# Mixture-of-experts blocks of 256 with a last block of 128 for experts that have at most 128 choices left

## The chip, the cores and the metric

The kernel runs on one core of a Trainium2 chip. The metric is device time in microseconds (us), the median of the runs shown. Before the change it is 2036.22 us, the median of three runs (2031.78, 2036.22 and 2037.07).

## The reference, cut to what matters

The network has four layers over 2708 nodes (rows of `x`) with 256 features each. Every layer is a graph step (a weighted sum over neighbours through the 2708 x 2708 matrix `adj`) followed by a feed-forward step. The change is in the feed-forward step of layer 0, a mixture of eight experts:

```python
def _L0_ffn_ref(x, Wg, bg, W1, b1, W2, b2):
    TOP_K = 2
    xf = x.reshape(-1, D)
    gate_logits = xf @ Wg + bg
    top_w, top_i = jax.lax.top_k(gate_logits, TOP_K)
    top_w = jax.nn.softmax(top_w, axis=-1)
    w_dense = jnp.sum(jax.nn.one_hot(top_i, E, dtype=xf.dtype) * top_w[..., None], axis=1)
    out = jnp.zeros_like(xf)
    for e in range(E):
        h = jax.nn.gelu(xf @ W1[e] + b1[e], approximate=False)
        out = out + w_dense[:, e:e + 1] * (h @ W2[e] + b2[e])
    return out.reshape(B, L, D)

# --- layer 0 ---
x = x + _L0_gnn_ref(_layernorm(x), adj, L0_gnn_W, L0_gnn_B)
x = x + _L0_ffn_ref((_layernorm(x))[None], L0_ffn_Wg, ...)[0]
# --- layer 1 ---
x = x + _L1_gnn_ref(_layernorm(x), adj, L1_gnn_W, L1_gnn_b)
...
```

Each row chooses two of the eight experts, so there are 2 x 2708 = 5416 choices, each of which needs one expert's two products (256 to 1024, gelu, 1024 to 256). Which expert gets how many choices depends on the data. The inputs come from a fixed seed. Layer 1's feed-forward step has one common hidden layer and lets every row choose one expert for the second product.

## The kernel before

Everything is float32. One matrix product of a 128 x 128 stationary tile is written as two TensorE instructions in the trace, so the 16 products of an expert block's first layer appear as 32 instructions.

**Layer 0's graph step** goes over the rows in three groups of 9, 7 and 6 tiles of 128 (`GROUPS`). After each group `send` normalizes its rows, computes the gate, chooses two experts per row, and `route` gives every choice a place in a list in memory (`taken0`) that is sorted by expert within the group. The rows, with their place in the output and their weight, are scattered to these places by indirect DMAs from GpSimd's queue.

**Planning.** `blocks` turns the counts per expert into a list of blocks. A block belongs to one expert and holds `B` of its choices (`B` = 256 in layer 0, two halves `k` of 128). For each block it computes the expert's number `ei` and, for every lane, the place `ix` in `taken0` from which its row is read. It is some thirty small VectorE instructions on all 128 partitions. It is called twice. Call "A" comes after the second group and makes `NA` = 9 blocks that are full with what is known by then. Call "B" (line 899) comes after the third group and makes `MOST - NA` = 20 blocks for the rest; the last block of each expert is filled up with lanes that point out of range, and their reads and writes are dropped. A 256-row block with 8 rows in it takes as much time as a full one.

**The expert stage.** `work0.run(hc, items, ...)` (line 935) is unrolled over the 9 blocks of "A" and the first `ALWAYS` = 15 blocks of "B". For each block:

- `fetch` (SyncE's queue) loads the two weight matrices of the block's expert, `wa` and `wb`, two blocks ahead; there are three buffers for each.
- `fetch_rows` (GpSimd's queue) gathers the two halves' rows into `xs`, three blocks ahead; for blocks of "B" VectorE first sets `xs` to ones.
- `turn` transposes the rows on TensorE (four transposes, line 545) and VectorE copies the result to `xTs` (line 551).
- The first layer: for each of 8 slices `f` of the hidden layer two products with 256 columns (line 578) and one gelu on ScalarE over 256 columns (line 580) into `hTs`, of which there is one buffer.
- The second layer: for each half `k`, 8 products with 256 columns (line 587), then bias and weight on VectorE (lines 589, 590), then a scatter of the 128 rows to `given0` from GpSimd's queue (line 481).

`beside(n)` puts other work between the blocks: sums of the columns of `adj`, which layer 1 needs (half rows `adhalf` are loaded on SyncE's queue and added on VectorE, line 925). At block 12 it also loads the number of blocks needed into a register on every engine (`blocks_left`).

`work0.run_rest` (line 937) then holds the five remaining blocks of "B" in a run-time `If`: they are computed only if more than 15 blocks of "B" are needed. After it come the column sums' product (line 942) and layer 1, whose first loads (`both`, line 991) wait until all scatters to `given0` have landed.

**The order of the work** on each engine is set by a scheduler that orders instructions by their place in the source and by when their inputs are free; a few dependencies written by hand ("order") hold things back. Instructions in the `If` are scheduled as one piece. [...]

The change also touches `run_rest` and the count for layer 1 (lines 1142 to 1159), where the blocks have 128 choices and nothing else changes.

Of the kernel before, what the change touches and what calls it, by code (L numbers as in the profile page):

```python
# [8 lines left out]
F32 = mybir.dt.float32  # L9
# [6 lines left out]
P = 128  # L16
N = 2708
# [49 lines left out]
def adj_ffn4(ctx: ExitStack, tc: tile.TileContext, a: dict, out: bass.AP):  # L67
# [326 lines left out]

    def blocks(pool, brief, known, NB, B, name, done=None, full=False):

# [114 lines left out]
    class Blocks:  # L511
# [15 lines left out]
        def fetch_rows(self, item):  # L527
            (_, ix, _), b, past, src, full = item
# [11 lines left out]
        def turn(self, pool, xs, after=None):  # L540
            xT = pool.tile([P, DC, 2 * P], F32, name="xTs", bufs=2)
            p = pools["psum"].tile([P, W], F32, name="turned", bufs=1)
            for k in range(2):
                for c in range(DC):
                    i = te.transpose(p[:, (c * 2 + k) * P : (c * 2 + k + 1) * P],
                                     xs[:, k, c * P : (c + 1) * P], ident)
                    if after is not None:
                        tc.add_manual_dep(i.ins, after, mybir.DependencyInfo(
                            mybir.DependencyClass.NoSync, mybir.DependencyReason.DATA),
                            reason="order")  # L550
            v.tensor_copy(xT.rearrange("p c t -> p (c t)"), p)
            return xT

        def run(self, pool, items, during=None, after=None):
# [9 lines left out]
            for n in range(len(items)):  # L564
                w1, bias, w2 = ahead.pop(0)
                xs, xT = self.rows.pop(0), turned
                if rows_todo:
                    self.fetch_rows(rows_todo.pop(0))
                if todo:
                    self.fetch(todo.pop(0))  # L570
                if during is not None:
                    during(n)
                hT = pool.tile([P, HC, 2 * P], F32, name="hTs", bufs=1)
                for f in range(HC):
                    if f % 2 == 0:
                        p = ps_acc().rearrange("p (k t) -> p k t", k=2)
                    for c in range(DC):
                        te.matmul(p[:, f % 2, :], lhsT=w1[:, c, f * P : (f + 1) * P],  # L578
                                  rhs=xT[:, c, :], start=(c == 0), stop=(c == DC - 1))
                    s.activation(hT[:, f, :], p[:, f % 2, :], AF.Gelu, bias=bias[:, f : f + 1])  # L580
                if self.rows:
                    turned = self.turn(pool, self.rows[0])
                y = pool.tile([P, 2, D], F32, name="ys", bufs=2)
                q = pools["psum"].tile([P, 2, D], F32, name="yacc", bufs=2)
                for k in range(2):
                    for f in range(HC):
                        te.matmul(q[:, k, :], lhsT=hT[:, f, k * P : (k + 1) * P], rhs=w2[:, f, :],  # L587
                                  start=(f == 0), stop=(f == HC - 1))
                    v.tensor_tensor(y[:, k, :], q[:, k, :], w2[:, HC, :], ALU.add)  # L589
                    v.tensor_scalar(y[:, k, :], y[:, k, :], xs[:, k, D + 1 :], None, op0=ALU.mult)  # L590
# [3 lines left out]
        def run_rest(self, pool, items, left, most):  # L594

            with tc.If(left > most):
                self.run(pool, items)
            pin(scattered[self.ok][-1].name)

    class Units(Blocks):  # L600
# [13 lines left out]
        def fetch_names(self, item):  # L614
            (_, ix, _), b, past, src, full = item
            m = self.names[:, self.places[0], :]
# [38 lines left out]
        def run(self, pool, items, during=None):  # L655
# [6 lines left out]
            while self.rows:  # L662
# [56 lines left out]
    held = sum(rows(t) for q in GROUPS[:-1] for t in q)  # L719
    NA, MOST = 9, (2 * N - E) // (2 * P) + E  # L720
    assert NA <= -(-(2 * held - E * (2 * P - 1)) // (2 * P))
    ALWAYS = 15
    with ExitStack() as l0:
# [102 lines left out]
        for tiles in GROUPS:  # L826
# [82 lines left out]
        halves = [(j, c0) for j in range(NT) for c0 in (0, N // 2)]  # L909

# [5 lines left out]
        def beside(b):  # L916


            if b == NA + 3:
                left.append(blocks_left(rest[2], MOST))  # L920
            while read:
# [4 lines left out]
            if b < 3:  # L926
                return
            while halves and len(read) < (3 if b < NA else 2):
                j, c0 = halves.pop(0)
                ad = hp.tile([P, N // 2], F32, name="adhalf", bufs=3)  # L930
# [4 lines left out]
        work0.run(hc, items, beside, gated[-3])  # L935
        assert not halves and not read
        work0.run_rest(hc, more, left[0], ALWAYS)

# [22 lines left out]
    with ExitStack() as l1:  # L961
# [104 lines left out]
        for tiles in GROUPS1:  # L1066
# [82 lines left out]
        def beside(b):  # L1149
            if b == NA + 4:  # L1150
                left.append(blocks_left(rest[2], MOST))
                as_bc = row_bc(work, "L2_gnn_attn_src", D, "elu_e")
# [5 lines left out]
        work1.run(hc, items, beside)  # L1158
        work1.run_rest(hc, more, left[0], ALWAYS)

# [570 lines left out]
```

## Time and profile before

One execution was profiled. Times of stages come from that execution.

| what | value |
|---|---|
| median of the runs | 2036.22 us |
| the profiled execution's own time | 2048.93 us |
| its span in the trace | 2047.2 us |
| TensorE busy | 1916.4 us (94%) |
| VectorE busy | 1103.8 us (54%) |
| first to last gelu of layer 0's experts (line 580) | 275.1 to 623.2 us |
| blocks in that stage | 24 (24 loads of `wa`, 192 gelus of 128 x 256) |
| indirect DMAs in it | 48 gathers into `xs`, 48 scatters to `given0` |
| granted TensorE clock, mean | 0.967 |

How to read it: in a timeline a row gives the start, the time, the engine, the line, the operation, output<-inputs and how many instructions it stands for. PE is TensorE's products, PEld its loading of the stationary tile, DVE VectorE, ACT ScalarE, POOL GpSimd, SPq SyncE's queue of DMAs. In brackets stands how long the engine was idle before and what ended that. The mean time of one product in the groups is a latency; products overlap, so a pace is read from the distance between starts.

### The profile page before, as it was taken

The numbers are of one execution on the slowest core, as the hardware profiler recorded it, in microseconds if no ns is written. First come the engines' busy times: TensorE is split into PE (matmuls) and PEld (weight loads), VectorE is DVE, ScalarE is ACT, GpSimd is POOL, SyncE is SP. The second block draws the span as 40 slices with busy tenths as digits, with TensorE's granted clock in tenths as the row PEclk, the third lists the DMA queues.
The fourth block names the chain that finished last, engine by engine and source line by source line (L and its number), as shares of the span: only waits on it lengthen the run. The fifth ranks groups of instructions, "written<-read, shape, count | busy, mean of one in ns | idle before, by whom it ended". The sixth has DMA issues, their size and how long they took to land.

```text
span 2047.2 us, 25961 instructions
## 1 busy us (share of the span) xinstructions
PE 1916.4 (94%) x9641; PEld 1374.6 (67%) x9641; DVE 1103.8 (54%) x2503; ACT 639.0 (31%) x1407; POOL 333.0 (16%) x369
## 2 busy tenths in 40 slices
PE   7999979999997999999796889999999999999997
PEld 5888868888886788878675768887576522232334
DVE  7687842543434333344341165555445588987876
ACT  8777722222224203022221152223234400120112
POOL 1004362333321000102345300000000000000000
PEclk9999979999998999999897999999899999999998
DMA  8435567877744343534666720000101000000000
GB/s 267 144 101 156 171 219 269 324 289 303 268 175 126 119 137 111 144 86 121 200 200 234 304 69 1 1 1 1 41 1 32 16 1 21 21 26 11 16 11 24
DMA packets 86960, 243.93 MB, mean 119 GB/s; under 512 B 17151, under 2 KB 40919, under 8 KB 77612
## 3 DMA queue, kind: packets, MB, share of 16 engines
q1 hardware_dynamic: 69596, 196.81, 29.0%
q0 software_dynamic: 17232, 45.38, 6.5%
q8 instruction: 79, 1.29, 0.3%
q14 instruction: 53, 0.43, 0.1%
HBM read 216.54 MB, written 28.97 MB: 120 GB/s over the span
## 4 chain that ended last, share of the span: by engine, by line
PE 55%; issue 5%; DMA 5%; DVE 4%; POOL 3%; ACT 2%; POOLq 0%; SPq 0%; DVEq 0%; ACTq 0%
PE num L1643 11%; PE ps_acc L1319 9%; PE acc L1124 8%; PE ps_tmp L347 7%; PE den L1654 6%; PE ps_acc L1495 3%; PE ps_tmp L241 3%; DMA given<-ys,xs 2%; PE ps_tmp L198 1%; PE ps_acc L241 1%; PE ps_tmp L1045 1%; POOL given L481 1%; POOL names L495 1%; PE yacc L674 1%; DMA adrow<-in_adjT 1%
## 5 line engine op out<-in xcount | busy, mean ns | idle before, releaser
L1638 DVE SCALAR_TENSOR_TENSOR e<-arena,G,mask 128x1024 f32<-128x1024 f32 (+2 forms) x264 | 294.2, 1150 | 41.1 <-PE den L1654 40.7
L1643 PE MATMUL num<-e,wh 128*64 128x512 f32 (+4 forms) x1056 | 240.9, 553 | 0.3 <-ACT L_gnn_W L1176 0.3
L1124 PE MATMUL acc<-sup,adrow 128*128 128x256 f32 x882 | 200.7, 385 | 2.8 <-DVE o L1076 1.5
L1319 PE MATMUL ps_acc<-hh,e 128*128 128x257 f32 x882 | 199.2, 382 | 2.0 <-ACT o L1264 2.0
L863 PE MATMUL acc<-msg,wt 128*128 128x256 f32 x882 | 198.1, 381 | 2.4 <-DVE x L886 1.2
L1124 PEld LDWEIGHTS acc<-sup,adrow 128*128 128x128 f32 x882 | 166.4, 192 | 31.0 <-issue 4.6
L578 PE MATMUL ps_acc<-xTs,wa 128*128 128x256 f32 x768 | 179.5, 387 | 6.1 <-issue 3.3
L863 PEld LDWEIGHTS acc<-msg,wt 128*128 128x128 f32 x882 | 165.2, 190 | 28.1 <-DVE wt L824 2.1
L1319 PEld LDWEIGHTS ps_acc<-hh,e 128*128 128x128 f32 x882 | 163.7, 190 | 29.6 <-ACT o L1264 5.0
L1643 PEld LDWEIGHTS num<-e,wh 128*64 128x64 f32 (+1 forms) x1056 | 73.9, 136 | 153.2 <-issue 119.9
L587 PE MATMUL yacc<-wb,hTs 128*128 128x256 f32 x768 | 175.5, 381 | 0.5 <-DVE ys L589 0.5
L580 ACT ACTIVATE hTs<-ps_acc,wa 128x256 f32<-128x256 f32 x192 | 90.8, 475 | 259.4 <-PE yacc L587 172.0
L578 PEld LDWEIGHTS ps_acc<-xTs,wa 128*128 128x128 f32 x768 | 142.1, 192 | 35.2 <-ACT hTs L580 5.3
L587 PEld LDWEIGHTS yacc<-wb,hTs 128*128 128x128 f32 x768 | 145.2, 191 | 20.3 <-DVE ys L589 0.9
L1654 PE MATMUL den<-e,wh 128*32 128x512 f32 (+4 forms) x1056 | 138.2, 553 | 0.0
L1313 DVE SCALAR_TENSOR_TENSOR e<-Rb,G,mask 128x640 f32<-128x640 f32 (+2 forms) x110 | 85.2, 775 | 92.8 <-PE ps_acc L1319 92.7
L199 ACT COPY xT<-ps_tmp 128x256 f32<-128x256 f32 x120 | 40.7, 364 | 276.5 <-PE ps_tmp L198 275.4
L1093 DVE TENSOR_SCALAR mask<-adrow 128x1024 uint8<-128x1024 f32 (+1 forms) x66 | 41.4, 630 | 134.5 <-DMA adrow<-in_adjT 134.5
L674 PE MATMUL yacc<-wb,hTs 128*128 128x256 f32 x384 | 94.7, 400 | 7.6 <-DVE ys L675 3.8
L589 DVE TENSOR_TENSOR ys<-yacc,wb 128x256 f32<-128x256 f32 x48 | 20.4, 424 | 134.3 <-PE yacc L587 134.3
L1654 PEld LDWEIGHTS den<-e,wh 128*32 128x32 f32 (+1 forms) x1056 | 30.9, 108 | 90.0 <-issue 86.7
L674 PEld LDWEIGHTS yacc<-wb,hTs 128*128 128x128 f32 x384 | 75.1, 202 | 19.2 <-DVE ys L675 4.1
(423 smaller groups left out, 2660.4 us busy)
## 6 DMA issues: line engine op xcount, KB each, us to landing
adhalf<-in_adjT SPq DMA_DIRECT2D x42, 677.0 KB
wb<-in_L_ffn_W2p SPq DMA_DIRECT2D x24, 1152.0 KB
wb<-in_L_ffn_Wdp SPq DMA_DIRECT2D x24, 1152.0 KB
wa<-in_L_ffn_W1b SPq DMA_DIRECT2D x24, 1028.0 KB
adrow<-in_adjT SPq DMA_DIRECT2D x42, 512.0 KB
adrow<-in_adjT SPq DMA_DIRECT2D x42, 320.0 KB
adrow<-in_adjT SPq DMA_DIRECT2D x21, 576.0 KB
hid<-hrow POOLq DMA_DIRECT2D x21, 512.0 KB
```

The source lines that it names most:

```text
L347: te.matmul(p[:, :w], lhsT=w1[:, c, f * P : (f + 1) * P], rhs=xnT[:, c, c0 : c0 + w], start=(c == 0), stop=(c == DC - 1))
L578: te.matmul(p[:, f % 2, :], lhsT=w1[:, c, f * P : (f + 1) * P], rhs=xT[:, c, :], start=(c == 0), stop=(c == DC - 1))
L580: s.activation(hT[:, f, :], p[:, f % 2, :], AF.Gelu, bias=bias[:, f : f + 1])
L587: te.matmul(q[:, k, :], lhsT=hT[:, f, k * P : (k + 1) * P], rhs=w2[:, f, :], start=(f == 0), stop=(f == HC - 1))
L674: te.matmul(q, lhsT=hT[:, f, :], rhs=w2[:, f, :], start=(f == 0), stop=(f == HC - 1))
L863: te.matmul(p[:q, n - pair[0], :], lhsT=wt[:, k : k + q], rhs=msg[:r, j, :], start=(j == 0 and n == pair[0]), stop=(j == FULL - 1 and n == ...
L1124: te.matmul(p[:q, n - pair[0], :], lhsT=ad[:, k : k + q], rhs=sup[:r, j, :], start=(j == 0 and n == pair[0]), stop=False)
L1313: v.scalar_tensor_tensor(e[:r, :w], Rb[:r, c0 : c0 + w], G[:r, j, :], mask[:r, j, c0 : c0 + w], op0=ALU.max, op1=ALU.mult)
L1319: te.matmul(p[:, : D + 1], lhsT=e[:, k : k + q], rhs=hh[:, j, :], start=(j == 0), stop=False)
L1638: v.scalar_tensor_tensor(e[:r, :w], Rb[:r, k, :w], G[:r, j, 2 * pair + k, :], mask[:r, j, c0 : c0 + w], op0=ALU.max, op1=ALU.mult)
L1643: te.matmul(num[k * DK : (k + 1) * DK, hf, :q], lhsT=wh[:r, j, 2 * pair + k, :DK], rhs=e[:r, h0 - c0 : h0 - c0 + q], start=(j == 0), stop= ...
L1654: te.matmul(den[z : z + Q, :q], lhsT=wh[:ri, i, 2 * pair + k, DK : DK + 1].to_broadcast([ri, Q]), rhs=e[:ri, h0 - c0 : h0 - c0 + q], start ...
```

## The change

Call "B" now leaves out an expert's last choices where they are at most 128 (`least=P`), and a third call, "C", makes blocks of 128 for these, one at most per expert. The rows' gather, the turn, the first layer, the gelu, the second layer and the scatter of such a block handle one half instead of two. Of "B" `ALWAYS` = 13 blocks are always computed, of "C" `HALVES` = 2. `count_left` computes by how many blocks of either kind the need exceeds these; if it exceeds them, the `If` computes everything left, which is now 3 blocks of 256 (`MOST` is 25) and 6 of 128. `blocks` returns its counts in float; the cast to an integer moves into `count_left`.

```diff
-    def blocks(pool, brief, known, NB, B, name, done=None, full=False):
+    def blocks(pool, brief, known, NB, B, name, done=None, full=False, least=0):
...
+            if least:
+                v.tensor_scalar(rest, rest, -float(least), None, op0=ALU.add)
-        c = pool.tile([P, E, most], F32, name="b_c")
+        c = pool.tile([P, E, most], F32, name="b_c", tag=f"b_c{most}")
...
-        used = pool.tile([P, 1], I32, name="b_used")
-        v.tensor_copy(used, end[:, E - 1 :])
-        return ei, ix, used
+        return ei, ix, end[:, E - 1 :], nb[:, :, 0]
...
-            for k in range(2):
+            for k in range(ix.shape[2]):
                 gather(xs[:, k, :], src, ix[:, b, k : k + 1], src.shape[0] - 1, self.ik, past)
-            self.rows.append(xs)
+            self.rows.append((xs, ix.shape[2]))
...
-            for k in range(2):
+            for k in range(n):
                 for c in range(DC):
                     i = te.transpose(p[:, (c * 2 + k) * P : (c * 2 + k + 1) * P],
...
-            v.tensor_copy(xT.rearrange("p c t -> p (c t)"), p)
+            v.tensor_copy(xT[:, :, : n * P], p.rearrange("p (c t) -> p c t", c=DC)[:, :, : n * P])
...
-                        te.matmul(p[:, f % 2, :], lhsT=w1[:, c, f * P : (f + 1) * P],
-                                  rhs=xT[:, c, :], start=(c == 0), stop=(c == DC - 1))
-                    s.activation(hT[:, f, :], p[:, f % 2, :], AF.Gelu, bias=bias[:, f : f + 1])
+                        te.matmul(p[:, f % 2, : m * P], lhsT=w1[:, c, f * P : (f + 1) * P],
+                                  rhs=xT[:, c, : m * P], start=(c == 0), stop=(c == DC - 1))
+                    s.activation(hT[:, f, : m * P], p[:, f % 2, : m * P], AF.Gelu,
+                                 bias=bias[:, f : f + 1])
...
-                for k in range(2):
+                for k in range(m):
                     for f in range(HC):
                         te.matmul(q[:, k, :], lhsT=hT[:, f, k * P : (k + 1) * P], rhs=w2[:, f, :],
...
-            with tc.If(left > most):
+            with tc.If(left > 0):
                 self.run(pool, items)
...
+    def count_left(pool, *what):
+        most = pool.tile([P, 1], F32, name="b_most", bufs=1)
+        v.memset(most, 0.0)
+        for used, made in what:
+            v.scalar_tensor_tensor(most, used, -float(made), most, op0=ALU.add, op1=ALU.max)
+        used = pool.tile([P, 1], I32, name="b_used", bufs=1)
+        v.tensor_copy(used, most)
+        return used
...
-    NA, MOST = 9, (2 * N - E) // (2 * P) + E
+    NA, MOST = 9, (2 * N + E * (P - 1)) // (2 * P)
-    ALWAYS = 15
+    ALWAYS, HALVES = 13, 2
...
-        rest = blocks(hw, hc, known, MOST - NA, 2 * P, "B", done=full[2])
+        rest = blocks(hw, hc, known, MOST - NA, 2 * P, "B", done=full[2], least=P)
+        twice = hw.tile([P, E], F32, name="twice")
+        v.tensor_tensor(twice, full[2], rest[3], ALU.add)
+        v.tensor_scalar(twice, twice, 2.0, None, op0=ALU.mult)
+        used = hw.tile([P, 1], F32, name="used")
+        v.tensor_copy(used, rest[2])
+        halves = blocks(hw, hc, known, E, P, "C", done=twice)
+        too_many = count_left(hw, (used, ALWAYS), (halves[2], HALVES))
...
-        items += [(rest, b, past, taken[0], False) for b in range(ALWAYS)]
-        more = [(rest, b, past, taken[0], False) for b in range(ALWAYS, MOST - NA)]
+        rest = [(rest, b, past, taken[0], False) for b in range(MOST - NA)]
+        halves = [(halves, b, past, taken[0], False) for b in range(E)]
+        items += rest[:ALWAYS] + halves[:HALVES]
+        more = rest[ALWAYS:] + halves[HALVES:]
...
-        work0.run_rest(hc, more, left[0], ALWAYS)
+        work0.run_rest(hc, more, left[0])
...
+        too_many = count_left(hw, (rest[2], ALWAYS))
...
-                left.append(blocks_left(rest[2], MOST))
+                left.append(blocks_left(too_many, MOST))
```

More of the change, by code (lines that the diff above doesn't have):

```diff
@@ L527, in fetch_rows @@
         def fetch_rows(self, item):
[L528 removed]
+            (_, ix, *_), b, past, src, full = item
             pool, bufs = (self.pool, 2) if self.at[1] % 5 < 2 else (self.late, 3)
@@ L535, in fetch_rows, with turn @@
                 v.memset(xs, 1.0)
-            for k in range(2):
+            for k in range(ix.shape[2]):
                 gather(xs[:, k, :], src, ix[:, b, k : k + 1], src.shape[0] - 1, self.ik, past)
-            self.rows.append(xs)
-        def turn(self, pool, xs, after=None):
+            self.rows.append((xs, ix.shape[2]))
+        def turn(self, pool, rows, after=None):
+            xs, n = rows
             xT = pool.tile([P, DC, 2 * P], F32, name="xTs", bufs=2)
             p = pools["psum"].tile([P, W], F32, name="turned", bufs=1)
-            for k in range(2):
+            for k in range(n):
                 for c in range(DC):
@@ L565, in run @@
                 w1, bias, w2 = ahead.pop(0)
-                xs, xT = self.rows.pop(0), turned
+                (xs, m), xT = self.rows.pop(0), turned
                 if rows_todo:
@@ L592, in run, with run_rest @@
                             self.given.shape[0] - 1, self.ok)
-        def run_rest(self, pool, items, left, most):
-            with tc.If(left > most):
+        def run_rest(self, pool, items, left):
+            with tc.If(left > 0):
                 self.run(pool, items)
@@ L614, in fetch_names @@
         def fetch_names(self, item):
-            (_, ix, _), b, past, src, full = item
+            (_, ix, *_), b, past, src, full = item
             m = self.names[:, self.places[0], :]
@@ L908, in adj_ffn4 @@
         left, read = [], []
-        halves = [(j, c0) for j in range(NT) for c0 in (0, N // 2)]
+        parts = [(j, c0) for j in range(NT) for c0 in (0, N // 2)]
         def behind_outputs(i):
@@ L927, in beside @@
                 return
-            while halves and len(read) < (3 if b < NA else 2):
-                j, c0 = halves.pop(0)
+            while parts and len(read) < (3 if b < NA else 2):
+                j, c0 = parts.pop(0)
                 ad = hp.tile([P, N // 2], F32, name="adhalf", bufs=3)
@@ L935, in adj_ffn4 @@
         work0.run(hc, items, beside, gated[-3])
-        assert not halves and not read
-        work0.run_rest(hc, more, left[0], ALWAYS)
+        assert not parts and not read
+        work0.run_rest(hc, more, left[0])
         for q, t0, t1 in ((P, 0, FULL), (LAST, FULL, NT)):
@@ L1150, in beside @@
             if b == NA + 4:
-                left.append(blocks_left(rest[2], MOST))
+                left.append(blocks_left(too_many, MOST))
                 as_bc = row_bc(work, "L2_gnn_attn_src", D, "elu_e")
@@ L1158, in adj_ffn4 @@
         work1.run(hc, items, beside)
-        work1.run_rest(hc, more, left[0], ALWAYS)
+        work1.run_rest(hc, more, left[0])
     def elu_add(o, t, q):
```

## The prediction

> **What bounds the kernel now.** I first read the busy time by stage, for the stage that the change shortens. Columns: the stretch, its length, busy time of PE, PEld, DVE, ACT and POOL with instruction counts, granted TensorE clock, DMA share, GB/s.
>
> ```profile
> 270.00:311.00 41.00, 34.96 (x147) 28.60 (x148) 14.45 (x63) 10.64 (x20) 26.38 (x31) 0.82 0.56 174
> 311.00:440.00 129.00, 128.86 (x614) 110.59 (x613) 50.55 (x71) 34.17 (x72) 41.63 (x34) 1.00 0.80 304
> ...
> 540.00:598.30 58.30, 58.01 (x275) 49.38 (x274) 22.27 (x32) 15.19 (x32) 18.54 (x14) 1.00 0.66 247
> 598.30:631.00 32.70, 31.99 (x149) 27.03 (x147) 7.68 (x14) 8.87 (x17) 5.96 (x5) 1.00 0.05 17
> ```
>
> From 311 to 631 us TensorE is never idle for more than a fraction of a us, at full clock; every other engine is idle half the time or more. TensorE is the bound, and the last 33 us have almost no DMA (0.05). Then I read one block in the timeline, TensorE's products alone, for the pace:
>
> ```profile
> 594.85 3.62 PE L587 MATMUL yacc<-wb,hTs 128*128 128x256 f32 x16
> ...
> 598.30 1.03 PE L578 MATMUL ps_acc<-xTs,wa 128*128 128x256 f32 x4
> ...
> 599.17 3.62 PE L587 MATMUL yacc<-wb,hTs 128*128 128x256 f32 x16
> ...
> 602.62 6.22 PE L578 MATMUL ps_acc<-xTs,wa 128*128 128x256 f32 x28
> ...
> 608.68 0.60 PE L545 MATMUL turned<-ident,xs 128*128 128x128 f32 x4
> ...
> 609.12 3.62 PE L587 MATMUL yacc<-wb,hTs 128*128 128x256 f32 x16
> ```
>
> The distance between starts is the pace. 16 products of 256 columns take 598.30 - 594.85 = 3.45 us, 0.216 each; 28 take 608.68 - 602.62 = 6.06 us, again 0.216; four transposes of 128 columns take 0.44 us, 0.110 each, half of it. A block is 32 x 0.216 + 0.44 + 2 x 3.45 = 14.27 us, which is the distance from 594.85 to 609.12. The last read is the end of the stage:
>
> ```profile
> 627.09 3.72 PE L587 MATMUL yacc<-wb,hTs 128*128 128x256 f32 x16 [0.52 <-DVE ys L589]
> ...
> 631.74 7.98 PE L942 MATMUL ps_tmp<-ones,cs 128*128 128x1 f32 x44 [0.93 <-PEq L596]
> ...
> 631.93 0.98 POOL L481 DMA_INDIRECT given<-ys,xs  x1 [3.26 <-DVE ys L590]
> ...
> 636.78 20.45 SPq L56 DMA_DIRECT2D both<-given  x11
> ```
>
> The last product ends at 630.8, the last scatter goes out at 631.9 and layer 1's first load at 636.8: this tail of 6 us follows the last block and moves with it.
>
> **How many blocks.** I ran the reference's arithmetic for layer 0 up to its top-2 choice. The experts get 703, 745, 677, 750, 610, 730, 681 and 520 choices. The nine "A" blocks take 2, 2, 2, 2, 1, 0, 0, 0 full blocks of these, leaving 191, 233, 165, 238, 354, 730, 681 and 520. In blocks of 256, rounded up, that is 1+1+1+1+2+3+3+3 = 15, exactly the old `ALWAYS`; that no further block ran (24 loads of `wa`) agrees. With the change the blocks of 256 are 1+1+1+1+1+3+3+2 = 13: expert 4 keeps 354 - 256 = 98 choices and expert 7 keeps 520 - 512 = 8, one block of 128 each. So 13 and 2 are just enough, the count left is 0 and the `If` is skipped. The nearest tip is expert 3: 750 choices, and from 769 it would need a block of 128 too. The smallest distance between any row's second and third logit is 0.00015, so rounding on the chip may move a choice or two, not 19.
>
> **What is removed.** Two blocks of 256 at the end become two of 128. For each:
> - second layer: one of two halves goes, 16 x 0.216 = 3.45 us;
> - turn: two of four transposes go, 0.22 us;
> - first layer: 32 products keep their number and their 32 weight loads, and go from 256 to 128 columns.
>
> For the last the question is whether a product of 128 columns is bound by its weight load. The nearest rows are layer 1's last pair of tiles, the same product with 148 columns, and beside it the gelus:
>
> ```profile
> 1034.37 4.19 PE L347 MATMUL ps_tmp<-xT,L_ffn_W 128*128 128x148 f32 x32
> ```
> ```profile
> L580 ACT ACTIVATE hTs<-ps_acc,wa 128x256 f32<-128x256 f32 x192 | 90.8, 475 | 259.4 <-PE yacc L587 172.0 <-PE ps_acc L578 85.0 <-remote 1.6
> ...
> L349 ACT ACTIVATE hT<-ps_tmp,b 128x148 f32<-128x148 f32 x8 | 3.1, 385 | 1.8 <-PE ps_tmp L347 1.0
> ```
>
> 32 products with 32 different weights take 4.19 us; without the last one's latency (289 ns, the shortest of that line) that is 3.90 over 31, 0.126 us, and 0.216 x 148/256 is 0.125. The pace goes with the columns. The transposes, each with its own 128 x 128 load, show 0.110 at 128. So the first layer goes from 6.91 to 32 x 0.110 = 3.52, and 3.39 us are saved. [...] I take the row, which has the same type and the same line of work.
>
> Each block saves 3.45 + 0.22 + 3.39 = 7.06 us, two 14.1. The wait of 0.52 us between the last block's halves goes with its second half: 14.6. Against it: a full block has four of the next block's products between its halves, which hides the start of the gelus; a half block has none. ScalarE needs about 0.37 us for 128 columns (from 0.475 at 256 and 0.385 at 148), TensorE 0.44 for the four products of a slice, so ScalarE keeps up, and three accumulator tiles give room for six slices. I take 0.3 us per block, from 0 to 1: net 14.0 us.
>
> The chances to be hidden elsewhere: the two scatters, two gathers and four small VectorE instructions that go too are not on this path. The 24 pairs of weights stay. The last goes out at 589.00 and from 594 on the DMA share is 0.11 or less; the earliest use of the last `wb` is now 602.6 + 3.1 + 0.2 + 3.5 + 3.5 = 613 us, 24 us after its issue. Without that cover each us of lateness would cost one.
>
> **What is added.** Call "C": 8 instructions for `vec` and 23 more; `least` 1, `twice` and `used` 3, `count_left` 4 where a cast was: 38 on VectorE. By the rows of call "B" small ones take 0.15 to 0.2 us (34 x 0.17 = 5.8); two of 448 elements take 0.6 each (0.53 at 360 in call "A") and two of 176 take 0.34 (layer 1's); in sum 7.7, less 0.7 because "B" shrinks from 20 to 16 blocks. VectorE before, by stretch:
>
> ```profile
> 281.00:290.30 9.30, 8.89 (x38) 1.00 0.47 146
> 290.30:311.00 20.70, 0.85 (x3) 0.84 0.67 217
> ```
>
> Call "B" fills 281 to 290; after it VectorE has 20 us with three instructions in them. "C" needs "B"'s counts (ready at 282.8), so it goes beside and after "B" and fits: cost 0. What waits behind it on VectorE: the second block's `xTs`, copied at 287.25 and first used near 311, and the first block's `ys` at 289.5 and 293.8, whose scatters stand in GpSimd's queue behind eleven others until 299.45. Both can be 5 us late for nothing. Without this cover it costs 7 us. Layer 1 gets two more small instructions (0.3 us) beside its own call "B", whose count is first read at the fourteenth block: 0. The register load at block 12 is the same one. A gain from the additions has no row; I exclude it. In sum -14.0 us: 2048.93 to 2034.9 for the profiled execution, which was 12.7 us above the median, and 2036.2 to **2022.2 us** for the median.
>
> **The rivals.**
> - *Half a block is not half* [...] For: no row has exactly this product with a gelu behind it. Against: the 148 column row. Chance 0.08.
> - *The planning is not hidden*: if "C" is put ahead of work that TensorE needs before 290, 7 us come back, 2029. For: the same stretch already has a clock of 0.82 and a TensorE idle of 3 us near 301. Chance 0.08.
> - *The end is set by the scatters*, not by TensorE. For: the chain of waits has this line:
>
> ```profile
> 603.91 32.41 DMA given<-ys,xs
> ```
>
>   If a scatter of 603.9 really landed at 636.3, shorter blocks would give nothing: 2036. Against: nearly nothing moves then (0.00 DMA share from 610 to 614 and 622 to 626), so it landed early, and the line is one wait for many scatters put down to a wrong one. Chance 0.05.
> - *Slower: the `If` runs.* If a 14th block of 256 or a third of 128 is needed, 3 blocks of 14.3 and 6 of 7.2 run, with a start of some 7 us for 2.2 MB of weights at 304 GB/s: 93 us for the 14 saved, 2115. It decides at the first block over; 19 choices are between. Chance 0.04.
>
> **Numbers.** My case has the chance 0.75. Below 0.3% (6.1 us) a measurement of this kernel can't tell a change from none. Faster: 0.75 + 0.08 and most of the second rival, 0.88; same: the scatters and the rest of the second, 0.07; slower: the `If` and some harm from shifted buffers, 0.05. Low end: 14.6 saved with no loss and the runs' scatter of some 4.5 us, 2017; I put it at 2016. High end: the planning's 7 us come back, 2030.
>
> **What would show it.** Two blocks at the end with 128-column products at 0.11 us, the second layer of 3.45 us once each; the last scatter some 14 us closer to the first block's start; VectorE busy from 281 to about 297 with TensorE's rows there unchanged; 22 full blocks and two short ones. I am wrong if the 128-column rows start 0.15 us or more apart, if the first block of "B" starts later, or if more than 24 pairs of weights are loaded.

## The result, and the profile after

The changed kernel takes **2025.81 us** (median of four runs, 2021.0 to 2026.34), beside 2036.64 us for the kernel before, run with it (2031.78 to 2040.77). The ratio is 0.9942, with a 95% interval from 0.9916 to 0.9969: 11 to 12 us are gone, and the interval lies outside the 0.3% that count as no change.

The profiled execution of the changed kernel is 2025.4 us long, at its median. The one of before was 2048.93, some 12 above its median. So these two traces differ by 23.5 us, twice what the change gives. What belongs to the change is read from a second profile of each (first experiment).

The end of the stage, TensorE's products alone in the timeline of the changed kernel (start, time, engine, line, operation, how many; in brackets the idle time before and what ended it):

```profile
588.22 3.62 PE L590 MATMUL yacc<-wb,hTs 128*128 128x256 f32 x16
591.68 0.83 PE L580 MATMUL ps_acc<-xTs,wa 128*128 128x128 f32 x6
592.36 3.72 PE L590 MATMUL yacc<-wb,hTs 128*128 128x256 f32 x16
595.92 2.72 PE L580 MATMUL ps_acc<-xTs,wa 128*128 128x128 f32 x22
598.48 0.38 PE L547 MATMUL turned<-ident,xs 128*128 128x128 f32 x2
...
602.67 3.00 PE L580 MATMUL ps_acc<-xTs,wa 128*128 128x128 f32 x24
605.50 0.60 PE L590 MATMUL yacc<-wb,hTs 128*128 128x256 f32 x2
605.93 1.05 PE L580 MATMUL ps_acc<-xTs,wa 128*128 128x128 f32 x8
606.83 3.19 PE L590 MATMUL yacc<-wb,hTs 128*128 128x256 f32 x14
611.80 8.49 PE L966 MATMUL ps_tmp<-ones,cs 128*128 128x1 f32 x44 [1.79 <-PEq L599]
```

Two short blocks are there: 64 products of 128 columns in the first layer, one half in the second layer each, and no wait within them. The pace is 2.56 us for 22 products (595.92 to 598.48), 0.116 us each, and 2.83 for 24 (602.67 to 605.50), 0.118. The same stage by stretches (columns as in the prediction's first view); the last row holds the second half of the last full block and the two short ones:

```profile
304.00:440.00 136.00, 135.50 (x645) 116.66 (x644) 54.10 (x76) 35.93 (x76) 48.69 (x40) 1.00 0.80 300
540.00:591.68 51.68, 50.78 (x242) 43.23 (x240) 18.18 (x26) 13.89 (x30) 12.32 (x9) 1.00 0.65 253
591.68:610.00 18.32, 18.32 (x115) 16.49 (x113) 5.61 (x9) 6.94 (x17) 4.00 (x3) 1.00 0.07 22
```

TensorE is idle for 0.5 and 0.9 us in the first two rows, and in the last not at all. With a DMA share of 0.07 there, hardly anything was still being loaded.

Where something was lost first is the first block. Its second half and VectorE beside it, from the timeline:

```profile
290.26 3.72 PE L590 MATMUL yacc<-wb,hTs 128*128 128x256 f32 x16 [1.36 <-DVE ys L592]
```
```profile
288.87 0.60 DVE L451 TENSOR_REDUCE b_of<-b_part 128x56 f32<-128x448 f32 x1
289.39 0.17 DVE L466 TENSOR_TENSOR b_row<-b_row,b_step 128x32 f32<-128x32 f32 x1
289.60 0.19 DVE L473 TENSOR_TENSOR b_step<-b_pos,b_of 128x32 f32<-128x32 f32 x1
289.71 0.16 DVE L454 TENSOR_TENSOR b_eb<-count,b_of 128x8 f32<-128x8 f32 x1
289.79 0.42 DVE L592 TENSOR_TENSOR ys<-yacc,wb 128x256 f32<-128x256 f32 x1
```

TensorE stood 1.36 us until VectorE had read the first half's accumulator at 290.21. In these rows that read starts at 289.79 only, behind the instructions of call "B" (tiles of 32 elements and more) mixed with those of "C" (8, 56 and 448 elements). The trace of before has no such wait. Its rows there:

```profile
289.21 1.03 PE L578 MATMUL ps_acc<-xTs,wa 128*128 128x256 f32 x4
290.07 3.65 PE L587 MATMUL yacc<-wb,hTs 128*128 128x256 f32 x16
```
```profile
289.54 0.42 DVE L589 TENSOR_TENSOR ys<-yacc,wb 128x256 f32<-128x256 f32 x1
```

The read ended at 289.96, while TensorE was still at four other products, and the second half started behind these.

The count of instructions on the two profile pages agrees with the working: 36 products fewer than before (9605, before 9641), which are 2 x 16 of the second layer and 2 x 2 transposes; 36 VectorE instructions more (2539, before 2503), which are 38 of the planning and 2 in layer 1 less the 4 of the two halves that are gone; 4 instructions fewer on GpSimd. No more than 24 blocks run.

### The profile page after: what moved, and what is told of

It reads as the page before. It is cut to its first block, busy times and chain, and to the rows that moved or that the text cites. A ratio compares the mean times of both kernels' runs of the same rounds, so it can differ in the third digit from the quotient of the medians.

```text
span 2023.7 us, 25917 instructions
## 1 busy us (share of the span) xinstructions
PE 1896.0 (94%) x9605; PEld 1360.7 (67%) x9605; DVE 1105.8 (55%) x2539; ACT 637.0 (31%) x1407; POOL 328.2 (16%) x365
## 4 chain that ended last, share of the span: by engine, by line
PE 53%; issue 5%; DMA 4%; DVE 4%; POOL 2%; ACT 1%; another core or an unknown queue 1%; POOLq 0%; SPq 0%; ACTq 0%; DVEq 0%
PE num L1668 11%; PE ps_acc L1344 9%; PE acc L1148 7%; PE ps_tmp L347 7%; PE den L1679 6%; PE ps_acc L1520 3%; PE ps_tmp L241 3%; DMA hs<-hid,names 1%; PE ps_tmp L198 1%; PE ps_acc L241 1%; POOL hs L628 1%; PE ps_tmp L1069 1%; DMA taken<-names,r_ix 1%; POOL names L496 1%
## 5 line engine op out<-in xcount | busy, mean ns | idle before, releaser
L580 PE MATMUL ps_acc<-xTs,wa 128*128 128x256 f32 (+1 forms) x768 | 171.5, 376 | 2.2 <-DVE xTs L553 2.2
L590 PE MATMUL yacc<-wb,hTs 128*128 128x256 f32 x736 | 167.4, 380 | 1.4 <-DVE ys L592 1.4
L582 ACT ACTIVATE hTs<-ps_acc,wa 128x256 f32<-128x256 f32 (+1 forms) x192 | 88.8, 466 | 246.3 <-PE yacc L590 166.3
L580 PEld LDWEIGHTS ps_acc<-xTs,wa 128*128 128x128 f32 x768 | 138.0, 192 | 28.8 <-DVE xTs L553 4.7
L590 PEld LDWEIGHTS yacc<-wb,hTs 128*128 128x128 f32 x736 | 137.5, 190 | 19.9 <-DVE ys L592 2.3
L677 PE MATMUL yacc<-wb,hTs 128*128 128x256 f32 x384 | 94.5, 399 | 7.5 <-DMA wb<-in_L_ffn_Wdp 4.3
L677 PEld LDWEIGHTS yacc<-wb,hTs 128*128 128x128 f32 x384 | 74.9, 202 | 19.6 <-DVE ys L678 3.7
L839 DVE SCALAR_TENSOR_TENSOR wt<-adrow,wt 128x640 f32<-128x640 f32 (+3 forms) x67 | 71.0, 1062 | 30.9 <-ACT wt L141 30.5
```

The source lines that it names most:

```text
L580: te.matmul(p[:, f % 2, : m * P], lhsT=w1[:, c, f * P : (f + 1) * P], rhs=xT[:, c, : m * P], start=(c == 0), stop=(c == DC - 1))
L582: s.activation(hT[:, f, : m * P], p[:, f % 2, : m * P], AF.Gelu, bias=bias[:, f : f + 1])
L677: te.matmul(q, lhsT=hT[:, f, :], rhs=w2[:, f, :], start=(f == 0), stop=(f == HC - 1))
```

## The experiments

They ran in three groups on two chips, the third group on the second chip. The kernel before, run with each group, has medians of 2049.25, 2049.32 and 2047.57 us there, more than the 2036.64 above. So all comparisons are ratios to the kernel before in the same group. The ratio on record is not exactly that of the two medians; the two differ by up to 1.4 per mille, most in the run with the planning alone.

**Both kernels again.** No edit.

> The kernel before, unchanged, for a second profile. My theory (the pause of TensorE from 297 to 304 us in the first profile belongs to that execution): this profile has no pause of more than 1 us there, and from the start of the first hidden layer to the last second-layer product it takes 350 to 353 us instead of 358; ratio 1.000. Rival (the pause belongs to the program): it is here again, 358 us.

> The changed kernel, unchanged, for a second profile and a narrower interval. My theory (two half blocks are worth 14.7 us, the planning costs 1 to 2 us): 12 to 14 us less than before, ratio 0.993 to 0.994. Rival (part of the gain is given back later): 9 us or less, ratio 0.996.

The kernel before against itself: 0.9998 (0.9982 to 1.0014). The changed one: 2036.31 us, **0.9945** (0.9923 to 0.9966). The spans of the two profiles are 2045.8 and 2034.9 us, 10.9 apart. A third profile of the changed kernel, with the third group, came with 0.9953 (0.9938 to 0.9967), span 2035.2:

> The changed kernel for a third profile, beside the other three on the same chip. Theory: ratio to before 0.9935 to 0.995; from the first hidden product to the first block's second half 17.9 to 18.4 us; from the second half of the second block to the last product 305.8 to 306.5 us. Rival (the first two profiles were chance): other values there.

With the second profiles I can say where the first pair's 23.5 us were. I cut layer 0's expert stage at four marks: S, the first product of the first layer (near 273); K, the start of the first block's second half; T, the start of the second block's second half; and U, the start of the second layer of block 22, the last block that is full in both kernels. E is the end of the last second-layer product.

| us | before, 1st and 2nd profile | after, 1st, 2nd and 3rd |
|---|---|---|
| S to K | 17.12, 16.86 | 18.30, 17.91, 17.98 |
| K to T | 21.68, 22.39 | **13.95**, 23.00, 22.54 |
| T to E | 319.06, 319.36 | 305.81, 306.45, 306.34 |
| of it, T to U | 283.10, 283.40 | 284.01, 284.65, 284.54 |
| of it, U to E | 35.96, 35.96 | 21.80, 21.80, 21.80 |
| TensorE's waits for `xTs` in T to U | 0.4, 0.7 | 1.4, 2.1, 1.6 |
| E to the first load of `both` | 5.97, 5.90 | 6.57, 6.47, 6.54 |
| layer 3's attention products, first to last | 395.8, 395.7 | 392.6, 392.6, 396.4 |

U to E holds the short blocks and is 14.16 us shorter, in all profiles alike. T to E is shorter by 13.0 only (319.2 less 306.2): in the full blocks ahead, which the change leaves as they were, TensorE waits about 1.2 us longer for the copy to `xTs`. The longest such wait, in the second profile of the changed kernel, TensorE and then VectorE:

```profile
371.35 1.13 PE L580 MATMUL ps_acc<-xTs,wa 128*128 128x256 f32 x4 [1.38 <-DVE xTs L553]
```
```profile
370.26 0.49 DVE L536 MEMSET xs<- 128x516 f32 x1 [4.96 <-DMA given<-ys,xs]
370.67 0.63 DVE L553 COPY xTs<-turned 128x512 f32<-128x512 f32 x1
```

In front of the copy VectorE stood 4.96 us to set a later block's `xs` to ones, until a scatter had landed. This comes back, larger, where the short blocks run first. Why it costs more than before is not shown.

K to T is one block period, 14.27 us when undisturbed. In both profiles of before and in two of the three after, it is 7 to 9 us longer: TensorE pauses between 294 and 304. I had expected this pause to belong to one execution; that was wrong. In the third profile of the changed kernel, in the timeline:

```profile
295.31 1.03 PE L580 MATMUL ps_acc<-xTs,wa 128*128 128x256 f32 x4
302.95 6.75 PE L580 MATMUL ps_acc<-xTs,wa 128*128 128x256 f32 x22 [6.62 <-ACT hTs L582]
```

In the first profile after, the pause was missing (26 products from 293.82 without a gap), and that is 7.7 us of the 23.5. Another 3.2 us are in layer 3, which the change doesn't touch. In this pair the clock was lower before; TensorE's rows in the timeline of before, then of after, with the same products:

```profile
1961.59 2.91 PE L1654 MATMUL den<-e,wh 128*32 128x384 f32 x14
```
```profile
1941.26 1.60 PE L1679 MATMUL den<-e,wh 128*32 128x384 f32 x14
```

And the stretches of before around them, where the granted clock (third value from the end) is 0.5 with TensorE busy without a gap, and one from the third profile of the changed kernel:

```profile
1960.00:1962.00 2.00, 2.00 (x9) 0.78 (x11) 0.31 (x2) 0.20 (x2) 0.00 (x0) 0.73 0.00 0
1962.00:1964.00 2.00, 2.00 (x14) 0.20 (x8) 1.06 (x3) 0.84 (x4) 0.00 (x0) 0.50 0.00 0
1966.00:1968.00 2.00, 2.00 (x9) 1.35 (x11) 0.73 (x4) 1.37 (x6) 0.00 (x0) 0.57 0.03 8
```
```profile
1816.00:1818.00 2.00, 2.00 (x12) 0.20 (x8) 2.00 (x5) 0.00 (x0) 0.00 (x0) 0.50 0.00 0
```

So the lower clock is not a matter of the kernel: in its third profile the changed kernel has it too, at another place, and layer 3's products take 396.4 us.

**The short blocks without the planning.** The second halves of blocks 5 and 14 of "B", which hold no rows, are not computed; the two blocks stand last. Call "C" is not made. Which blocks are short is written into the kernel as constants, for these inputs alone.

```diff
+        first = (rest[0], rest[1][:, :, 0:1])
+        SHORT = (5, 14)
...
+        items += [whole[b] for b in range(ALWAYS) if b not in SHORT]
+        items += [(first, b, past, taken[0], False) for b in SHORT]
```

> Two half blocks at the end without the planning of blocks of 128: blocks 5 and 14 of the 15, whose second halves are empty with these inputs, are put last and done as halves by a fixed list. My theory: 14 to 15 us less than before, 1 to 2 us less than the changed kernel, and the second half of the first block starts without the wait of 1.4 us. Rival (the planning is hidden): the same as the changed kernel within 0.5 us.

2034.74 us, 0.9939 (0.9915 to 0.9963). T to E is 305.4 us, and the first block's second half starts with no wait put down to VectorE (290.93, S to K 17.37). The short blocks alone give the whole gain. The 1.6 us to the changed kernel's 2036.31 have the size of the planning's wait, but lie within the intervals.

**The planning without the short blocks.** Calls "B" and "C" and the count are made, and 15 blocks of 256 run as before.

```diff
-        items += rest[:ALWAYS] + halves[:HALVES]
-        more = rest[ALWAYS:] + halves[HALVES:]
+        items += rest[:ALWAYS]
+        more = rest[ALWAYS:]
```

> The planning of blocks of 128 without their use: 15 blocks of 256 as before, and the third planning call and the count beside them. My theory: 1 to 2 us more than before, lost at the second half of the first block, where TensorE waits for VectorE. Rival (the planning is hidden): as before within 0.5 us. Rival (the planning costs all of its VectorE time): 7 us more.

2042.82 us, **0.9983** (0.997 to 0.9996): 1.7 per mille faster where a small loss was expected. The profile has the wait (1.63 us, S to K 18.48) and no shorter block (T to E 319.5). So its gain isn't in the work that this edit touches. Of what the profile does show, 3.1 us are layer 3's products at full clock (392.6 us beside 395.7), 1.4 us an earlier S (272.39 beside 273.83) and 2.6 us a shorter pause from K to T (19.81 beside 22.39). None of these three is a known effect of the planning, and layer 3's clock and the pause differ between profiles of one kernel as well. I read from it that ratios here can differ by some 3 us for reasons outside the edit, and that a cost of 1.5 us can be shown as a wait in the trace, but not as a ratio.

**The planning later.** Call "C" is moved into the work beside block 2 of the stage, the count with it.

```diff
-        halves = blocks(hw, hc, known, E, P, "C", done=twice)
-        too_many = count_left(hw, (used, ALWAYS), (halves[2], HALVES))
...
+            if b == 2:
+                ...
+                planned.extend(blocks(hw, hc, was_known, E, P, "C", done=twice))
+                counted.append(count_left(hw, (used, ALWAYS), (planned[2], HALVES)))
```

> The changed kernel with the third planning call moved into the work beside block 2, where VectorE has little to do. My theory (the planning costs 1.2 us because the first block's second half waits for VectorE's read of its first half): that wait is gone and the first block's second half starts 17.0 to 17.4 us after the first hidden product, as in the kernel before, instead of 17.9 to 18.3; in all 1 us less than the changed kernel, ratio to before 0.994. Rival (the later start comes from another cause): still 17.9 us or more.

**Two accumulators.** The first half's and the second half's products go into tiles of their own, so the second half doesn't wait until VectorE has read the first.

```diff
-                q = pools["psum"].tile([P, 2, D], F32, name="yacc", bufs=2)
                 for k in range(m):
+                    q = pools["psum"].tile([P, W], F32, name="yacc", bufs=2)[:, None, :D]
```

> The changed kernel with an accumulator tile of its own for each half in place of one for both. My theory: the second half no longer waits for VectorE's read of the first, so the planning costs nothing: 17.0 to 17.4 us to the first block's second half, and 1 us less in all. Rival (the wait is for VectorE in another way): 18 us as in the changed kernel.

Late planning: 2031.57 us, 0.9917 (0.989 to 0.9945). Two accumulators: 2032.25 us, 0.9926 (0.9899 to 0.9952). First the place in the timeline with the planning late, TensorE and then VectorE:

```profile
274.40 4.96 PE L580 MATMUL ps_acc<-xTs,wa 128*128 128x256 f32 x12 [2.38 <-DVE xTs L553]
...
290.01 1.03 PE L580 MATMUL ps_acc<-xTs,wa 128*128 128x256 f32 x4
291.16 3.72 PE L590 MATMUL yacc<-wb,hTs 128*128 128x256 f32 x16
```
```profile
289.99 0.62 DVE L448 TENSOR_TENSOR b_part<-b_hot,b_vec 128x448 f32<-128x448 f32 x1
...
290.69 0.42 DVE L592 TENSOR_TENSOR ys<-yacc,wb 128x256 f32<-128x256 f32 x1
```

The wait is not listed any more, and S to K is 16.76 us, as before the change. But this edit does not show the mechanism. In the source "C" stands later; on VectorE most of it, the 448 elements too, still runs in front of the read. What differs is the start: in this profile TensorE waited 2.38 us for its first `xTs` (0.78 in those of before and after), so S came 1.6 us later beside VectorE's work, and the read was just in time. Now with two accumulators:

```profile
286.03 1.03 PE L580 MATMUL ps_acc<-xTs,wa 128*128 128x256 f32 x4
286.89 5.34 PE L590 MATMUL yacc<-wb,hTs 128*128 128x256 f32 x24
```
```profile
292.37 0.42 DVE L592 TENSOR_TENSOR ys<-yacc,wb 128x256 f32<-128x256 f32 x1
```

The first 8 of the 24 instructions end the first half, so the second half starts near 288.6, some 3.7 us before VectorE reads the first half, and TensorE doesn't wait. (S to K is 14.3 us here and can't be set beside the others, because products of block 2 moved behind K.) So the mechanism is shown: the wait of 1.4 to 2.3 us is there with "C" and without short blocks, not there with short blocks and without "C", and gone with "C" when the second half doesn't depend on the read. Its worth isn't pinned down: by ratio the two edits are 3.9 to 5.7 us better than 0.9945, and the intervals overlap. With two accumulators the waits for `xTs` after 311 us are gone too (0.7 us are left with the planning late), so their gain isn't the one wait alone. Both together, in the group with the third profile of the changed kernel:

> The changed kernel with both edits that take away the wait at the first block: the third planning call beside block 2 and an accumulator tile for each half. My theory: 1 to 3 us less than the changed kernel on the same chip, ratio to before 0.991 to 0.993. Rival (the wait is given back in the pause near 300 us that follows it in nearly all profiles): the same as the changed kernel within 0.5 us.

2029.23 us, **0.9916** (0.9888 to 0.9944), the changed kernel beside it 0.9953. This is the best ratio of all, and its profile is without the wait: products of the second layer have no idle time before them (0.0 us; 1.4 in the changed kernel), and E comes at 613.0 us instead of 620.6. Some 3 us of this 7.6 are a shorter pause from 294 on (gaps of 3.3 us beside 6.6), which may be chance; 1.6 us are waits for `xTs` that are gone. That it beats the kernel before is clear. Against the changed kernel the intervals overlap a little.

**The short blocks first.** They run ahead of the 13 full ones of "B", not behind.

```diff
-        items += rest[:ALWAYS] + halves[:HALVES]
+        items += halves[:HALVES] + rest[:ALWAYS]
```

> The changed kernel with the two half blocks right behind the nine A blocks instead of at the end. My theory (at the end the halves need no weights that are not there; in the middle each half block of 7.2 us needs 2.2 MB, 7.3 us at 300 GB/s, beside the half rows of adj): TensorE waits there for weights, 2 to 6 us of the 13 saved are lost, ratio to before 0.995 to 0.997. Rival (the place does not matter): as the changed kernel, 0.9943, with no wait for weights of more than 0.5 us.

2048.0 us, **0.9995** (0.9979 to 1.001): nothing of the gain is left, where I had expected to lose less than half. I had thought of weights that come late, since two short blocks in the middle give the loads behind them half the time. The trace names another cause. TensorE, then VectorE in the timeline, then the stretches:

```profile
427.91 3.62 PE L590 MATMUL yacc<-wb,hTs 128*128 128x256 f32 x16
439.68 9.87 PE L580 MATMUL ps_acc<-xTs,wa 128*128 128x256 f32 x32 [8.15 <-DVE xTs L553]
```
```profile
437.12 0.49 DVE L536 MEMSET xs<- 128x516 f32 x1 [9.21 <-DMA given<-ys,xs]
437.53 1.50 DVE L949 TENSOR_TENSOR cs<-cs,adhalf 128x1354 f32<-128x1354 f32 x1
438.95 0.68 DVE L553 COPY xTs<-turned 128x512 f32<-128x512 f32 x1
```
```profile
424.00:432.00 8.00, 7.53 (x50) 6.62 (x48) 2.60 (x4) 2.83 (x8) 4.33 (x3) 1.00 1.01 419
432.00:440.00 8.00, 0.32 (x1) 0.32 (x2) 2.84 (x5) 0.00 (x0) 1.58 (x1) 0.68 0.74 299
440.00:450.00 10.00, 10.00 (x37) 8.26 (x37) 3.00 (x4) 3.72 (x8) 3.43 (x3) 0.74 0.58 213
```
```profile
434.00:435.00 1.00, 0.00 (x0) 0.00 (x0) 0.00 (x0) 0.00 (x0) 0.00 (x0) 0.97 1.02 408
445.00:446.00 1.00, 1.00 (x6) 0.90 (x5) 0.00 (x0) 0.47 (x1) 0.00 (x0) 0.91 1.03 422
```

VectorE sets a later block's `xs` to ones. That waits 9.21 us for the scatter that still reads this buffer, while the share of the DMA engines is 1.01 (419 GB/s, 424 to 432) and 1.02 (434 to 435). Behind it on VectorE stands the copy to `xTs` (438.95), and TensorE stands 8.15 us for that. After the stop TensorE's clock is 0.74 in the next stretch, and 32 products take 9.7 us (439.68 to 449.39) instead of 6.9. In stretches of 1 us the clock leaves 1.00 between 434 and 435 (0.97), 2.5 to 3.5 us after the last product ended (431.53). It is back at full between 445 and 446 (0.91 there), over 5 us after the restart at 439.68, and 2.8 us are lost to it. To test what VectorE's order does, I left the order of the blocks and let GpSimd set the ones:

```diff
-                v.memset(xs, 1.0)
+                g.memset(xs, 1.0)
```

> The two half blocks right behind the A blocks, as in the earlier run, and the setting of xs to ones on GpSimd instead of VectorE. My theory now (there VectorE stood 9.2 us at the setting of xs, which waits until the scatter of an earlier block has landed, and the copy to xTs that TensorE needs stood behind it): the wait of 8.2 us for xTs is gone or under 1.5 us, the clock stays at 1.00, and most of the lost 10 us come back, ratio to before 0.995 to 0.997. Rival (the weights are late): TensorE waits there as long, now for wa or wb, ratio 0.9995.

2032.84 us, 0.9926 (0.9901 to 0.995). The same place in its timeline:

```profile
428.09 3.62 PE L590 MATMUL yacc<-wb,hTs 128*128 128x256 f32 x16
431.55 7.09 PE L580 MATMUL ps_acc<-xTs,wa 128*128 128x256 f32 x32
```

No wait, and the gain is back, more of it than expected (0.995 to 0.997): cause shown. The share of the DMA engines is no lower than it was (1.01 and 1.02 from 424 to 440), so a share of 1.0 alone doesn't stop TensorE here, and my theory of the weights falls. From 311 us to the last block no wait for `xTs` is left at all, and T to E is 303.95 us, 2.3 less than in the changed kernel, so the ones on VectorE probably cost that something too. This order with the other edits is untested.

**A third short block.** One more, whose rows are all out of range, always runs.

```diff
-    ALWAYS, HALVES = 13, 2
+    ALWAYS, HALVES = 13, 3
```

> The changed kernel with a third half block, which is empty with these inputs. My theory: 7.2 to 7.6 us more than the changed kernel, 32 products of 128 columns at 0.116 us, 16 of 256 at 0.216, two transposes: 7.4 us from the last full block's end; ratio to before 0.998. Rival (a half block has a price beside its products, such as a start of the gelus that nothing hides): 8.5 us or more.

2045.39 us, 0.9986 (0.9966 to 1.0007), which is 0.0041 or 8 us above the changed kernel's 0.9945; the intervals of these two just touch. Its profile is sharper: the starts of the last groups of the three short blocks (608.27, 615.41 and 623.02) lie 7.1 and 7.6 us apart, and U to E is 29.35, 7.55 more than with two. A short block costs half of 14.27 us, with no fixed part beyond 0.5 us, as expected (7.2 to 7.6).

**One short block, so that the `If` runs.** This measures the prediction's rival on the slow side.

```diff
-    ALWAYS, HALVES = 13, 2
+    ALWAYS, HALVES = 13, 1
```

> The changed kernel with one half block outside the run-time If, so that with these inputs the If runs: 3 blocks of 256 and 7 of 128, of which one half block holds rows. Theory (the price of the rival on the slow side): 3 x 14.3 + 7 x 7.4 less one half block of 7.4, and 7 to 10 us for the first weights: 94 to 100 us more than the changed kernel, ratio to before 1.040 to 1.044. Rival (in the If the weights of each half block hold it up, 2.2 MB per 7.4 us): 110 us more or above.

2139.49 us, **1.045** (1.0418 to 1.0483): 92 us slower than before and 101 slower than the changed kernel in the same group, a little over the 94 to 100 expected. TensorE at the branch:

```profile
606.89 2.75 PE L590 MATMUL yacc<-wb,hTs 128*128 128x256 f32 x12
617.09 1.09 PE L547 MATMUL turned<-ident,xs 128*128 128x128 f32 x4 [7.43 <-DMA xs<-taken,b_ix]
```

Nothing in the `If` is loaded ahead, and it starts with 7.43 us of waiting for rows. `both` is loaded at 720.9 us instead of 627.2. The change rests on the counts of these inputs, and this is what being one block short costs.

## Why the prediction was right, and which step failed

The forecast was 2022.2 us in a range from 2016 to 2030, and 2025.81 came out. The main mechanism held; of the 14.0 us that the sum gave, 11 to 12 arrived. What was removed was worth what the prediction said. Three costs that it put at nothing took 2.9 us of it.

- **How many blocks.** Right. 24 blocks ran, two of them short, 24 pairs of weights; the `If` was skipped.
- **What is removed: 7.06 us a block, less 0.3 for the gelus, and the 0.52 us wait.** Right: U to E is 14.16 us shorter, 14.0 were forecast. Two small errors nearly cancel here, which is luck. The pace of the 128-column products is 0.116 to 0.118 us, not 0.110, so 64 of them take some 0.45 us more than worked out; and the 0.6 us set aside for the gelus were not needed, for no product of the short blocks waits.
- **The full blocks ahead stay as they are.** The prediction took this for granted, and it failed by 1.2 us: T to U is that much longer, which is what TensorE waits longer for `xTs`. It had named harm from shifted buffers only among the chances of a slower kernel.
- **The pace of a product of 128 columns, taken from the rows.** The rows decided rightly. Worked out were 0.110 us a product, as in the transposes; measured were 0.116 to 0.118, where 256 columns take 0.216. The rival "half a block is not half" is refuted.
- **The tail of 6 us moves with the last block.** Nearly. It grew from 5.9 to 6.5 us. TensorE's wait for its sequencer there is 1.7 to 1.8 us in the changed kernel; with a full block last it was 0.8 to 0.9 (before) and 0.4 to 0.6 (the short blocks first, in both versions). So it goes with the short block at the end. Why is not shown.
- **"C" fits beside and after "B": cost 0. Both can be 5 us late for nothing.** This step failed. I counted VectorE's time as free and looked only at who waits for `ys`' scatter. VectorE's read of the accumulator also frees it for TensorE: the first half's read had 0.1 us of slack before (it ended at 289.96, the second half started at 290.07), not 5. The prediction had shown the same wait at the last block (0.52 us, put down to `ys`) without drawing this from it. "C"'s instructions, mixed in with "B"'s, held the read up, and TensorE stood 1.4 to 2.3 us. Two accumulators removed this. S to K grew by less, 1.1 us (18.1 beside 17.0), because before TensorE also did four transposes there that now come later, and stood 0.6 to 1.5 us ahead of them until VectorE had copied the transposes before. The rival "the planning is not hidden" was thus right in kind and too large with 7 us: most of it is covered.
- **The scatters set the end.** Refuted. In the chain of waits the 32.41 us line is again a wait for an unknown or wrongly named queue, and `both` is still loaded 6.5 us after the last product, with T to E 13 us shorter:

```profile
589.47 26.67 another core or an unknown queue
617.76 7.61 DMA both<-given
```

- **The weights' cover of 24 us.** Held with the short blocks last: nothing waits for weights.
- **Slower: the `If`.** Didn't happen. As a price, 79 us over the kernel before were worked out and 92 measured, with one short block less outside the `If` and one more inside than in the rival.
- **The sum.** 14.2 from the short blocks, less 1.2 for the waits for `xTs`, 1.1 from S to K and 0.6 for the tail: 11.3 us, and 11.3 by the ratio of the second profiles' group (0.9945). The spans of these profiles differ by 10.9; that this is so near is in part luck, for 3.1 us of it are layer 3's clock, and 4.4 the other way lie between the first load of `both` and layer 3 (986.1 us before, 990.5 after; 989.0 and 989.2 in the first pair), where the change adds two small instructions only.
- **Before's own profile.** The sum was carried over to the median by the difference alone, which was right: the part that the change shortens, T to E, took the same in both profiles of before (319.06 and 319.36 us).

Open is the pause of TensorE between 294 and 304. It is in nearly every profile of both kernels and takes about 3 to 12 us, as much as the whole gain. The products wait for gelus, but these are not the start of it. In the second profile of the changed kernel VectorE's read of the second half's accumulator stands as well, and both start together at 301.1 to 301.2 us, as they do at 302.4 in the third. The product that both need is drawn as ended some 7 us earlier, and the trace names no releaser for either ("remote"). In the first profile of before VectorE read in time (293.76), and 3.28 us of TensorE's pause have no cause that the trace names ("issue"). No experiment here tests it.

## What to carry to other kernels

An engine with idle time isn't free at every moment (VectorE was busy for 54% of the span before, and with "C" on it TensorE stood 1.4 to 2.3 us for one read): for each instruction that added work goes ahead of, ask what buffer it frees and who writes that buffer next, and not only who reads its result. When work is cut into smaller pieces, look at what refills their buffers, and on which engine the first write of the refill waits: here it stood 9.21 us on VectorE, with the copy that TensorE needed behind it, and TensorE stood 8.15 us. It was enough to run the small pieces last, or to move that write to another engine. And profile both kernels again before two traces are subtracted: here one pair showed 23.5 us for a change worth 11.

## What was not expected of the hardware

TensorE's granted clock fell to 0.5 for some 7 us (about 1961 to 1967 in the profile of before) in a stretch in which TensorE was busy without a gap; the same products ran at 1.0 in the first profile of after. Most stationary tiles there have 32 or 64 columns (30 of the 36 products in the rows from 1960.81 to 1969.58). In stretches of 1 us from 1930 to the fall TensorE is busy 1.00 in each, so no stop like the one of 8.15 us stands in the 31 us ahead of it; what sets the fall off is open. It is in 6 of the 14 profiles, in the kernel before, in the changed one and in variants, at more than one place of layer 3, and costs 2 to 7 us there (394.6 to 399.4 us for products that take 392.6 to 392.9 without it). With the pause near 300 it is a reason why two profiles of one kernel differ by some us.
